# Second cross-attention of a two-block diffusion transformer: the first output product of a batch element issued behind the next element's sums and turned rows

## The chip, the cores and the metric

One core of one Trainium2 chip runs the whole program. The metric is the device time of one execution in microseconds, taken as the median of several executions. The profile shown is that of one execution of its own.

## What is computed

Eight batch elements of 512 tokens with 256 channels run through two transformer blocks. The part that this document is about is the cross-attention of the second block, with 16 heads of 64 channels and 64 context tokens for each element:

```python
cross_in = _adaln(x, cond, ln1_w, ln1_b, g1_w, g1_b, b1_w, b1_b)
ctx_n = _ln(context, ca_lnc_w, ca_lnc_b)
x = _attn(cross_in, ctx_n, ca_wq, ca_wkv, ca_wo, ca_bo) + x
...
q = _rope(_heads(xq @ wq), sq, cq);  k = _rope(_heads(ctx @ wk), sk, ck)
a = softmax(einsum('bhnd,bhmd->bhnm', q, k) * DH ** (-0.5))
o = einsum('bhnm,bhmd->bhnd', a, v).transpose(...).reshape(b, n, MID)
return o @ wo + bo
```

Everything is float32. Before this part come the first block and the second block's self-attention; after it comes the second block's feed-forward.

## The kernel before, in words

The order of the instructions on TensorE, VectorE, ScalarE and GpSimd is written out by hand: within `manual_schedule` (L1397) each of these engines issues its instructions in the order in which the Python code names them. Only the queue of SyncE, which starts nearly all transfers, is ordered by the compiler.

The cross-attention is `cross()` (L1334). It loops over the batch elements b and, in each, over eight steps j = 0..7. One pair of heads fills the 128 partitions, so there are eight pairs (NPAIR). The pieces that a step puts together are these:

- `queries(n)` (L1226): the queries of one pair, two matmuls of 512 columns into a PSUM tile, then rotary embedding in `rope_pair` (L840 to L844): three VectorE multiplications that read the PSUM tile (one at L840, two at L843), and one GpSimd addition that makes the query tile. The call at step j makes the queries for three steps ahead.
- `outer(b, pp)` (L1215): values times the output weight, copied to `vw` by ScalarE. With that, output weight and values are one factor, and the last product of the attention is probabilities times `vw`.
- `score(b, pp)` (L1236): the scores of two pairs, and their exponential on ScalarE (L1243) into a tile `p`. The probabilities are not yet divided by their sum.
- `sums(b, half)` (L1245): the sums of half the heads, four matmuls with a selecting matrix into one PSUM tile, a ScalarE copy `den` (L1253), and transfers (L1256, L1258) that bring them into a dense layout.
- `inverse(b, half)` (L1260): the reciprocal on VectorE (L1263), a transfer out (L1265), and eight transfers (L1270) that spread the reciprocals over the partitions as four tiles `rb`.
- `scaled(b, half)` (L1272): four multiplications of `p` by `rb` (L1277), two on GpSimd and two on VectorE in turn.
- `cross_out(b, t)` (L1290): the output of 128 tokens, eight matmuls of 256 columns with the eight scaled tiles `p` as weights and `vw` as the moving operand, through `out_tile` (L1279) and `project_tile` (L450). Products 0 and 1 share one PSUM tile, which is taken at product 0; products 2 and 3 share another. Behind product 1 and behind product 3 VectorE adds the tile to `x` (`add_to`, L461; L464).
- `turn(i)` (L1208): the normalised rows of the next element are turned by eight TensorE transposes in two groups, each into a PSUM tile of its own (L427), which ScalarE scales into `hT` (L428). The queries of the next element need `hT`.

The output products of element b-1 are issued in the steps of element b: product 0 and sums and turn at step 4, product 1 at the head of step 5, product 2 at step 6, product 3 at step 7. The scaling of the second half of b-1 is issued at step 3.

PSUM tiles of one bank come from `bank_x()` (L106), which goes round four banks by a counter: the single bank of tag D, the single bank of tag O, and twice tag X, which has two banks. Every `queries`, `outer`, `sums` and every group of `turn` takes one tile from it, and so do products 0 and 2. A tile can be taken only when what its bank held before has been read; the framework makes TensorE wait for that reader. For tag X the framework hands out the one of the two banks that has been given back first. Scores have four banks of their own (tag S).

```python
def bank_x():
    turns[0] += 1
    n = turns[0] % (2 + len(extra))
    if n < len(extra):
        return extra[n]()          # bank_d, bank_o
    return psum.tile([P, 512], F32, tag="X", name="ps_X", bufs=2)
```

Of the kernel before, what the change touches and what calls it, by code (L numbers as in the profile page):

```python
# [85 lines left out]
def fast_path(ctx: ExitStack, tc: tile.TileContext, a: dict, out: bass.AP):  # L86
# [334 lines left out]
    def transposed(pool, z, b, am, bm, bufs=2):  # L421

        hT = pool.tile([P, 2, N], F32, tag="hT", name="hT", bufs=bufs)
        for k in range(2):
            ps = bank_x()
            for t in range(NT):
                nc.tensor.transpose(ps[:, t * P : (t + 1) * P], z[:, t, k * P : (k + 1) * P], ident)  # L427
            nc.scalar.activation(hT[:, k, :], ps, AF.Identity, bias=bm[:, k, b : b + 1], scale=am[:, k, b : b + 1])  # L428
        return hT
# [512 lines left out]
    def load_kb(b):  # L942
        for i in range(4):
            r = slice(32 * i, 32 * i + 32)
            nc.sync.dma_start(kvs[b % 2][0][r, :, i % 2, :], k_d[r, :, b, :])

    def load_vb(b):
        for e in range(2):
            r = slice(64 * e, 64 * e + 64)
            nc.sync.dma_start(kvs[b % 2][1][r, :, e, :], v_d[r, :, b, :])  # L950
# [236 lines left out]
    with tc.tile_pool(name="ph5", bufs=2) as wk:  # L1187
# [9 lines left out]
        def rows_(i, n=None):  # L1197

            if i < 2 * B:
                b = i % B  # L1200
                if not n:
                    pieces[i] = normed_in_pieces(nk, b, EPS1, lambda z: turned_rows.update({i: z}))
                for piece in pieces[i] if n is None else pieces[i][n : n + 1]:
                    piece()
                if n in (None, 2):
                    add_row(b, row("ffb2" if i // B else "cabo"))

        def turn(i):  # L1208
            if i < 2 * B:
                am, bm = ((a1, b1), (a2, b2))[i // B]  # L1210
                turned_rows[i] = transposed((nk, wk)[i % 2], turned_rows[i], i % B, am, bm, 1)
# [3 lines left out]
        def outer(b, pp):  # L1215

            s = ss[b]
            if pp == 0:
                s["vw"] = wk.tile([P, NPAIR, D], F32, tag="vw", name="vw")
            ps = bank_x()  # L1220
            for i in range(2):
                p = 2 * pp + i
                mm(ps[:, i * D : (i + 1) * D], kvs[b % 2][1][:, p, :, :].rearrange("p e k -> p (e k)"), w_co[:, p, :])
            nc.scalar.copy(s["vw"][:, 2 * pp : 2 * pp + 2, :], ps.rearrange("p (i d) -> p i d", i=2))

        def queries(n):  # L1226
            b, p = divmod(n, NPAIR)
            if b == B:
                return
            ps = bank_x()  # L1230
            for k in range(2):
                mm(ps, w_cq[:, k, p * P : (p + 1) * P], turned_rows[b][:, k, :], k == 0, k == 1)
            ss[b][p] = q = wk.tile([P, N], F32, tag="q", name="q", bufs=7)
            rope_pair(wk, ps[:, None, :], rope_c[:, None, :], rope_s2[:, None, :], [P, 1, N], q[:, None, :])

        def score(b, pp):  # L1236
            s = ss[b]
            ps = bank_s()
            for i in range(2):
                p = 2 * pp + i  # L1240
                mm(ps[:, i, :], kvs[b % 2][0][:, p, :, :].rearrange("p e k -> p (e k)"), s[p])
            s["p", pp] = pr = wk.tile([P, 2, N], F32, tag="p", name="p", bufs=8)
            nc.scalar.activation(pr, ps, AF.Exp, scale=HD1 ** -0.5)  # L1243

        def sums(b, half):  # L1245

            s = ss[b]
            d = bank_x()
            for j in range(4):
                p = 4 * half + j  # L1250
                mm(d[32 * j : 32 * j + 32, :], sel0, s["p", p // 2][:, p % 2, :])
            den = wk.tile([P, N], F32, tag="den", name="den", bufs=1)
            nc.scalar.copy(den, d)  # L1253
            dd = dram.tile([4, 2, N], F32, tag="den5", name="den5")
            for e in range(2):
                nc.sync.dma_start(dd[:, e, :], den.rearrange("(j r) n -> j r n", j=4)[:, e, :])  # L1256
            s["rec", half] = rec = wk.tile([P, 8 * N // P], F32, tag="rec", name="rec")
            nc.sync.dma_start(rec, flat(dd))  # L1258

        def inverse(b, half):  # L1260
            s = ss[b]
            rec = s["rec", half]
            nc.vector.reciprocal(rec, rec)  # L1263
            rd = dram.tile([4, 2, N], F32, tag="rec5", name="rec5")
            nc.sync.dma_start(flat(rd), rec)  # L1265
            check(rec)
            for j in range(4):
                s["rb", j] = rb = wk.tile([P, N], F32, tag="rb", name="rb", bufs=4)
                for e in range(2):
                    nc.sync.dma_start(rb[64 * e : 64 * e + 64, :], rd[j, e : e + 1, :].to_broadcast([64, N]))  # L1270

        def scaled(b, half):  # L1272
            s = ss[b]
            for j in range(4):
                p = 4 * half + j
                pr = s["p", p // 2][:, p % 2, :]
                (nc.gpsimd, nc.vector)[p % 2].tensor_tensor(pr, pr, s["rb", j], ALU.mult)  # L1277

        def out_tile(b, t, lhsT, w):  # L1279
            s = ss[b]  # L1280
            if t % 2 == 0:
                s["ps"] = bank_x()
            project_tile(s["ps"], t % 2, lhsT, w, 8, t)
            if b == B - 1 and w is w_f2 and t > 1:
                x = xs[b][:, t, :]
                nc.vector.tensor_tensor(x, s["ps"][:, (t % 2) * D : (t % 2 + 1) * D], x, ALU.add)
            elif t % 2:
                add_to(b)(t // 2, s["ps"].rearrange("p (j d) -> p j d", j=2))

        def cross_out(b, t):  # L1290
            out_tile(b, t, lambda k: ss[b]["p", k // 2][:, k % 2, :], ss[b]["vw"])
# [42 lines left out]
        def cross():  # L1334
            LEAD = 3
            for n in range(LEAD):
                queries(n)
                if n:
                    outer(0, n - 1)
            for z in kvs[1]:  # L1340
                nc.gpsimd.memset(z, 0.0)
            for b in range(B):
                for j in range(NPAIR):
                    if j % 2 == 0:
                        queries(NPAIR * b + j + LEAD)
                        score(b, j // 2)
                    if b and j in (5, 6):
                        cross_out(b - 1, j - 4)
                    if j % 2:
                        queries(NPAIR * b + j + LEAD)  # L1350
                    if j < 2:
                        for pp in (2 * j, 2 * j + 1) if b else (2 + j,):
                            outer(b, pp)
                    if b:
                        if j == 0:
                            scaled(b - 1, 0)
                        if j == 1:
                            inverse(b - 1, 1)
                        if j == 3:
                            scaled(b - 1, 1)  # L1360
                        if j in (4, 7):
                            cross_out(b - 1, j - 4)
                    if j == 2 and b + 1 < B:
                        load_kb(b + 1)
                        load_vb(b + 1)
                    if j == 4:
                        sums(b, 0)
                        turn(b + 1)
                    if j > 4:
                        rows_(b + 2, j - 5)  # L1370
                    if j == 6:
                        inverse(b, 0)
                    if j == 7:
                        sums(b, 1)
# [22 lines left out]
        with tc.manual_schedule(engines={ENG.PE, ENG.DVE, ENG.Activation, ENG.Pool}):  # L1397
            cross()
            return feed_forward()
# [865 lines left out]
```

## Time and profile before

| what | us |
|---|---|
| median of 3 runs (lowest, highest) | 2419.1 (2417.03, 2423.43) |
| the profiled execution, its own time | 2413.91 |
| span of the profile | 2411.8 |
| TensorE busy in the span | 2379.0 |
| from the first product of element 0 (issued in element 1) to the first product of element 6 (issued in element 7), start to start | 257.7 |

The granted TensorE clock was 0.998 of full speed. In the profile a matmul in float32 appears as two records. The groups of the output products carry the name `ps_O<-vw,p` or `ps_X<-vw,p`, by the bank they write, the sums `<-p,sel`, the transposes `<-ident,z`, and the queries `<-hT,w_ca_wq`. Their line is L116, the helper that issues every matmul, or L427 for transposes. A number in square brackets in the timeline is the idle time of the engine ahead of an instruction, with what ended it.

### The profile page before, as it was taken

How to read it: one execution, taken by the hardware profiler on the slowest of the kernel's cores; microseconds unless marked ns; L12 is line 12 of the kernel's file. 1: busy time of each engine (PE TensorE's matmuls, PEld its weight loads, DVE VectorE, ACT ScalarE, POOL GpSimd, SP SyncE). 2: the span in 40 equal slices, each digit the busy share in tenths (PEclk: the TensorE clock that was granted, in tenths of full speed). 3: DMA queues.
4: the chain of work that ended last, by engine and by line, in shares of the span. 5: the costliest groups of instructions: out<-in, count | busy, mean ns of one | idle time of the engine just before them, and what ended most of it. 6: DMA issues, size and time to landing. Idle time of an engine off the chain costs nothing.

```text
span 2411.8 us, 28553 instructions
## 1 busy us (share of the span) xinstructions
PE 2379.0 (99%) x10964; PEld 1158.8 (48%) x10964; DVE 1139.5 (47%) x2115; ACT 889.2 (37%) x1118; POOL 966.5 (40%) x588
## 2 busy tenths in 40 slices
PE   9999999999999999999999999999999999999998
PEld 4333544544545633434343444444445556567665
DVE  4564534434345344555454555545445656651110
ACT  4665545545442134333333333333342212221221
POOL 4563323323201046555555554646453445441110
PEclk9999999999999999999999999999999999999999
DMA  5130000000002001000101010100023212210000
GB/s 184 33 107 11 16 15 13 16 14 6 12 11 92 0 1 32 14 24 10 28 10 28 10 28 10 28 10 26 30 67 95 77 58 68 64 56 31 18 22 20
DMA packets 84897, 84.07 MB, mean 35 GB/s; under 512 B 42656, under 2 KB 59792, under 8 KB 84752
## 3 DMA queue, kind: packets, MB, share of 16 engines
q1 hardware_dynamic: 83208, 78.99, 11.0%
q8 instruction: 88, 1.44, 0.2%
q0 software_dynamic: 640, 2.10, 0.2%
q10 hardware_dynamic: 904, 1.07, 0.2%
q14 instruction: 57, 0.47, 0.1%
HBM read 72.09 MB, written 10.04 MB: 34 GB/s over the span
## 4 chain that ended last, share of the span: by engine, by line
PE 87%; DVE 4%; POOL 3%; issue 3%; DMA 1%; ACT 1%; SPq 1%; POOLq 0%; DVEq 0%; ACTq 0%
PE ps_X L116 36%; PE ps_S L116 22%; PE ps_D L116 13%; PE ps_O L116 13%; PE ps_X L427 1%; DMA rb<-rec 1%; DVE t L843 1%; POOL x L448 1%; DVE sm L1039 1%; POOL p L1277 1%; ACT p L590 0%; PE ps_X L610 0%; POOL var L561 0%; DVE t L1000 0%; SPq L1270 0%
## 5 line engine op out<-in xcount | busy, mean ns | idle before, releaser
L116 PE MATMUL ps_S<-q,k 32*128 32x512 f32 (+1 forms) x3072 | 425.6, 623 | 5.5 <-ACT p L590 3.4
L1020 ACT ACTIVATE p<-ps_S 128x1024 f32<-128x1024 f32 x256 | 250.8, 1022 | 459.7 <-PE ps_S L116 450.3
L590 ACT ACTIVATE p<-ps_S 128x1024 f32<-128x1024 f32 x256 | 248.3, 1022 | 171.6 <-PE ps_S L116 170.3
L116 PEld LDWEIGHTS ps_S<-q,k 32*128 32x128 f32 (+1 forms) x3072 | 148.7, 183 | 244.8 <-issue 155.5
L1039 DVE TENSOR_TENSOR sm<-sm,p 128x1024 f32<-128x1024 f32 x128 | 252.1, 2028 | 0.1
L999 DVE TENSOR_TENSOR t<-ps_X,rope_c 128x512 f32<-128x512 f32 x126 | 87.0, 690 | 341.0 <-PE ps_X L116 341.0
L1002 POOL TENSOR_TENSOR q<-t 128x512 f32<-128x512 f32 x32 | 65.5, 2047 | 294.3 <-DVE t L1000 294.3
L182 POOL TENSOR_TENSOR rstd<-rstd,mhalf 128x4 f32<-128x4 f32 x49 | 51.2, 1044 | 293.6 <-DVE rstd L181 292.6
L844 POOL TENSOR_TENSOR q<-t,t 128x512 f32<-128x512 f32 x72 | 94.9, 1319 | 172.6 <-DVE t L843 171.6
L116 PE MATMUL ps_X<-hT,w 128*128 128x512 f32 x328 | 151.0, 597 | 0.5 <-DVE t L780 0.5
L1035 POOL TENSOR_TENSOR sm<-p 128x1024 f32<-128x1024 f32 x64 | 149.7, 2364 | 1.9 <-ACT p L1020 1.9
L1085 POOL TENSOR_TENSOR oT<-oT,rb 128x512 f32<-128x512 f32 x63 | 128.9, 2065 | 19.6 <-DMA rb<-rec_d 19.6
L116 PE MATMUL ps_O<-p,v 128*64 128x512 f32 x512 | 134.9, 605 | 0.0
L116 PE MATMUL ps_D<-p,v 128*64 128x512 f32 x512 | 131.6, 592 | 0.0
L116 PE MATMUL ps_O<-p,h 128*32 128x512 f32 x1024 | 129.5, 609 | 0.6 <-ACT p L590 0.6
L621 POOL TENSOR_TENSOR attn<-attn,gate 128x256 f32<-128x256 f32 x32 | 23.3, 727 | 250.7 <-DVE attn L619 250.7
L116 PE MATMUL ps_X<-w_sa_wv,hT 128*128 128x512 f32 x256 | 118.0, 604 | 0.0
L1002 POOL TENSOR_TENSOR k<-t 128x512 f32<-128x512 f32 x32 | 40.7, 1272 | 192.8 <-DVE t L1000 192.8
L116 PE MATMUL ps_X<-hT,w_sa_wq 128*128 128x512 f32 x256 | 115.9, 595 | 0.0
L116 PE MATMUL ps_X<-w_sa_wo,oT 128*128 128x256 f32 x512 | 114.5, 382 | 0.1
L116 PE MATMUL ps_X<-hT,w_sa_wk 128*128 128x512 f32 x248 | 114.6, 605 | 0.0
L116 PE MATMUL ps_S<-hT,w_ff_w 128*128 128x512 f32 x256 | 111.3, 593 | 0.0
(286 smaller groups left out, 3663.6 us busy)
## 6 DMA issues: line engine op xcount, KB each, us to landing
rb<-rec SPq DMA_DIRECT2D x128, 128.0 KB
rb<-rec_d SPq DMA_DIRECT2D x124, 128.0 KB
rb<-rec SPq DMA_DIRECT2D x16, 256.0 KB
out_dram<-x SPq DMA_DIRECT2D x15, 256.0 KB
x<-in_x_dram SPq DMA_DIRECT2D x7, 512.0 KB
gate<-modd SPq DMA_DIRECT2D x24, 128.0 KB
k_d<-q POOLq DMA_DIRECT2D x8, 256.0 KB, 2.4
v_d<-v SPq DMA_DIRECT2D x8, 256.0 KB
```

The source lines that it names most:

```text
L116: nc.tensor.matmul(o, lhsT, rhs, start=start, stop=stop)
L182: nc.gpsimd.tensor_tensor(r[:, :n], r[:, :n], mhalf[:, :n], ALU.pow)
L427: nc.tensor.transpose(ps[:, t * P : (t + 1) * P], z[:, t, k * P : (k + 1) * P], ident)
L448: nc.gpsimd.tensor_tensor(xs[b], xs[b], r[:, None, :].to_broadcast([P, NT, D]), ALU.add)
L590: nc.scalar.activation(pr[u], pss[u], AF.Exp, scale=HD0 ** -0.5)
L844: nc.gpsimd.tensor_tensor(dst, t1, t2, ALU.add)
L999: nc.vector.tensor_tensor(c, ps, rope_c, ALU.mult)
L1002: nc.gpsimd.tensor_tensor(r[0], ec, os, ALU.subtract)
L1020: nc.scalar.activation(pr, pss[u], AF.Exp, scale=HD1 ** -0.5)
L1035: nc.gpsimd.tensor_tensor(sm, s["p", g, 0, u], s["p", g, 1, u], ALU.add)
L1039: nc.vector.tensor_tensor(s["sm", g, u], s["sm", g, u], s["p", g, t, u], ALU.add)
L1085: eng.tensor_tensor(o, o, s["rb", g, u], ALU.mult)
```

## The change

Product 0 of element b-1 moves, within step 4 of element b, from ahead of `sums(b, 0)` and `turn(b + 1)` to behind them. Product 1 stays at the head of step 5 and so comes straight behind it. No instruction is added or taken away, and all other pieces keep their places. This holds for the seven elements b = 1..7; the products of the last element are issued in `feed_forward()` and are as they were.

```diff
                         if j == 3:
                             scaled(b - 1, 1)
-                        if j in (4, 7):
-                            cross_out(b - 1, j - 4)
+                        if j == 7:
+                            cross_out(b - 1, 3)
                     if j == 2 and b + 1 < B:
                         load_kb(b + 1)
                         load_vb(b + 1)
                     if j == 4:
                         sums(b, 0)
                         turn(b + 1)
+                        if b:
+                            cross_out(b - 1, 0)
                     if j > 4:
                         rows_(b + 2, j - 5)
```

## The prediction, on record before the result was known

> **What bounds the kernel now.** I read first the busy times, then TensorE's waits in the stage of the change (1825 to 2165 us), then the timeline of one element, because what the change is worth is decided there.
>
> ```profile
> PE 2379.0 (99%) x10964; PEld 1158.8 (48%) x10964; DVE 1139.5 (47%) x2115; ACT 889.2 (37%) x1118; POOL 966.5 (40%) x588
> ```
>
> TensorE is busy in 99% of the span and everything else in less than half: a microsecond that TensorE stalls is a microsecond of the kernel, unless it was waiting there anyway. The waits of TensorE in the stage (total, times, longest):
>
> ```profile
> PE ps_O L116 <- DVE x L464: 2.6, 3, 0.9
> PE ps_O L116 <- POOL p L1277: 2.1, 5, 0.9
> PE ps_X L116 <- DVE t L843: 1.7, 1, 1.7
> PE ps_X L116 <- POOL p L1277: 1.1, 4, 0.5
> ```
>
> Two waits recur. Product 0 waits for the scaled tiles (`p L1277`), and something behind product 1 waits for VectorE's addition to `x` (L464). Matmul ends are modelled, so I size both by start times. The timeline of element 2, TensorE first, then VectorE:
>
> ```profile
> 1929.64 1.88 PE L116 MATMUL ps_S<-q,kv 128*128 128x512 f32 x4
> 1931.36 1.89 PE L116 MATMUL ps_X<-vw,p 128*128 128x256 f32 x8
> 1933.43 2.48 PE L116 MATMUL ps_X<-vw,p 128*128 128x256 f32 x8 [0.18 <-POOL p L1277]
> 1935.83 1.07 PE L116 MATMUL ps_D<-p,sel 128*32 128x512 f32 x8
> 1936.83 0.66 PE L427 MATMUL ps_O<-ident,z 128*128 128x128 f32 x4
> 1937.42 0.63 PE L427 MATMUL ps_X<-ident,z 128*128 128x128 f32 x4
> 1937.89 3.62 PE L116 MATMUL ps_X<-vw,p 128*128 128x256 f32 x16
> 1941.34 1.88 PE L116 MATMUL ps_X<-hT,w_ca_wq 128*128 128x512 f32 x4
> ```
> ```profile
> 1931.55 0.70 DVE L1277 TENSOR_TENSOR p<-p,rb 128x512 f32<-128x512 f32 x1 [1.25 <-DMA rb<-rec]
> 1933.51 1.64 DVE L1277 TENSOR_TENSOR p<-p,rb 128x512 f32<-128x512 f32 x1 [1.26 <-DMA rb<-rec]
> 1935.18 0.69 DVE L840 TENSOR_TENSOR t<-ps_X,rope_c 128x512 f32<-128x512 f32 x1
> 1935.89 1.39 DVE L843 TENSOR_TENSOR t<-ps_X,rope_s 64x512 f32<-64x512 f32 x2
> 1941.54 0.69 DVE L464 TENSOR_TENSOR x<-ps_X,x 128x512 f32<-128x512 f32 x1 [4.27 <-PE ps_X L116]
> ```
>
> To be seen: product 0 (16 records) takes 4.47 us from its start to the start of the sums, product 1, which waits for nothing, 3.45 us; so product 0 stalls 1.02. And VectorE is late here. Its scaling waits for the `rb` transfers, and behind it in the queue stands the rotary embedding (L840, L843) of the step's own queries, whose PSUM tile is read out only at 1937.28, although TensorE filled it before 1929.64.
>
> **What the Trainium skill says.** "PSUM — Partial Sum Buffer", section "PSUM bank collisions raise a hardware error": accesses of two engines to a bank must be kept apart by semaphores, by bank and not by address; so a new tile in a bank waits for the last reader of the old one. The trace agrees: at element 1 the queries at 1899.13 in bank O start 0.15 us after the addition that read bank O ended (1898.98). "TensorE: Matmul & The Clock Gate", section "The mechanism": matmuls start and end in program order; so a matmul that waits for a bank holds up all behind it. The trace shows no matmul overtaking. "Perfetto Trace Analysis", section "Matmuls": independent groups should rotate through PSUM banks so that the evacuation of one overlaps the next group; here the rotation is where the change bites. "SBUF — State Buffer", section "SBUF: two separate sides": VectorE with two SBUF inputs and GpSimd exclude each other on a shared port. The trace agrees: L1277 on VectorE takes 0.70 above, and 1.64 beside GpSimd's L1277.
>
> **The change, part by part.** Let S be the start of product 0 before, for element b; all else is relative to it.
>
> (1) The order on TensorE. Sums take 1.00 us (1935.83 to 1936.83), the transposes 1.06 (to 1937.89). Moved ahead, they begin at S: their inputs are old, and they end at S+2.06. No DMA is moved past anything on TensorE; the `den` copy, its transfers and `hT` start about 4.4 us earlier, and nobody waits for them before (VectorE's L1263 for this half has no listed wait, and the queries that need `hT` come behind product 1), so I count nothing.
>
> (2) The wait for scaled tiles. The last of them is ready at S+3.79 typically (S+4.93 at element 1), and product 0 needs it at its eighth matmul, 7 x 0.43 = 3.0 us after its start. A start at S+2.06 would be late enough. This stall goes. Start to next start, product 0 takes 5.61, 4.47, 4.71, 4.47, 4.48, 4.80, 4.46 us in elements 1 to 7; less 3.45 each that is 8.9 us.
>
> (3) The bank. This is the part that decides. `bank_x` goes round four banks. From the fourth tile back before step 4 the takers are: the last `outer`, queries of step 2, of step 3, of step 4; then before the change: product 0, sums, transposes 1, transposes 2. So the last transposes reuse the bank of step 4's queries, at S+6.06 in element 2, when VectorE has just done with it. After the change it is sums, transposes 1, transposes 2, product 0: **product 0 takes the bank of the queries of step 4**. In the trace those queries write D in odd elements, where product 0 would then be the D tile, and X in even ones, where of the two X banks the sums get the one given back first. Sums and transposes get banks read out before S (the queries of step 3 by S-1.06, S-0.44 at element 1).
>
> So product 0 can start only at E+0.15, where E is the end of the last L843 for the queries of step 4, and 0.15 is the hand-over measured above. From the VectorE timelines, E is S+7.06, 5.92, 6.15, 5.92, 5.92, 4.69, 5.91. What makes E is not moved: VectorE's queue has scaling, then L840 and two L843 (2.1 us together), in the same order, and the scaling waits for `rb`. TensorE thus stands still from S+2.06 to S+6.07 typically, 4.0 us, and product 0 with its 3.45 us lies wholly behind it, where before most of it lay beside VectorE's lateness. Behind it on TensorE wait product 1, the next queries and the scores, so all of the kernel.
>
> Product 1 then ends at E+0.15+6.90; before, it ended at S+T+2.06+3.45, with T the times of (2). The difference is E+1.54-T: 2.99, 2.99, 2.98, 2.99, 2.98, 1.43, 2.99, in all **19.3 us lost**.
>
> (4) The other bank. In odd elements product 0 and 1 held O, and the queries of step 5 came round to O and waited for the addition: product 1 takes 4.49 to its next start there instead of 3.45, in elements 1, 3 and 5 (element 7 has no further queries). That is 3 x 1.04 = **3.1 us gained**, since these queries now get the bank of the sums, read out long before. In even elements they waited for nothing already (1941.34, ahead of the addition at 1941.54).
>
> (5) What follows. VectorE sits idle 4.27 us ahead of the addition in each element; the delay shifts TensorE and VectorE together from there, so the chain of reciprocal and `rb` for the next element starts as late as its products, and the loss comes again in each element without growing. Nothing else is added.
>
> Sum: 19.3 - 3.1 = 16.2 us slower. On the profiled execution that is 2413.9 + 16.2 = 2430.1. That execution lies 5.2 us under the median of the runs, so on the median I forecast 2419.1 + 16.2 = **2435.3 us**. A measurement of this kernel can tell about 0.3% (7 us) from no change.
>
> **Bounds.** E is the one uncertain time. At best `rb` lands as early as in element 6 and no L1277 of VectorE meets one of GpSimd: with 0.70 + 2.1 from S+1.4, E is S+4.2, the loss 1.3 an element, and 7 x 1.3 - 3.1 = 6 us: 2425. At worst the sums, not product 0, get the late X bank in three even elements, and product 0 comes another 2.06 us later: +6.2, 2441.5.
>
> **The rivals.** *Faster*: product 0's bank is free in time, because the bank is handed out otherwise than I count. Then (2) and (4) stand alone: 8.9 + 3.1 = 12.0 us gained, 2407.1. For it speaks that TensorE's listed waits name the scaled tiles and not this bank; against it, that before the change transposes 2, which hold the bank by my count, start 0.14 us behind E in element 2 and 0.59 behind transposes 1, but only 0.50 behind them in element 6 (2108.16 to 2108.66), where E is early: a tenth of the bank's wait shows. It decides at E = S+2.93 (S+3.97 where (4) helps): below, the change gains. E is 4.69 at the least. *No change*: E comes down by some 2.4 us on average, for instance since transfers land earlier behind a longer stall, and loss and gain cancel: 2419. Against it: reciprocal and `rb` issue lie ahead of the stall. *Much slower*: the stall feeds back into the order of SyncE's queue, which the compiler makes anew, and `rb` comes later by 2 us an element: 14 us more, 2449.
>
> **Chances.** Forecast 0.81, faster rival 0.07, no change 0.05, much slower 0.07. The range runs from under the lower bound to above the upper one with some room for the median's own scatter of 3 us: 2424 to 2443. Faster by over 0.3%: 0.07. Within 0.3%: 0.06. Slower by over 0.3%: 0.87.
>
> **What would show it.** Right: in each element TensorE idles about 4 us ahead of the first `<-vw,p` behind the transposes, put down to `DVE t L843`; product 0 then takes 3.45 us; the sums start at S; in odd elements product 0 writes D, and the wait for `DVE x L464` is gone; the step from one element's first product to the next grows by 2 to 3 us from about 42.8. Wrong: an idle time there under 1 us, or one put down to `POOL p`, or VectorE's L843 of step 4 ending well ahead of S+5.

## The result, and the profile after

Nine executions of the changed kernel have a median of 2437.3 us, nine of the kernel before 2419.37; the ratio, taken over all executions and not over the two medians (which would give 1.0074), is 1.0057, with a 95% interval of 1.0036 to 1.0077, so the change costs 9 to 19 us. The gains and losses of whole executions below are taken from such ratios. The profiled execution of the changed kernel took 2430.07 us, with a span of 2427.8 against 2411.8. Executions of the changed kernel range from 2425.5 to 2439.1 us, in step with their mean granted TensorE clock: 0.995 at 2425.5, 0.992 at 2429 to 2430, 0.989 to 0.990 at 2437 to 2439.

The waits of TensorE in the stage, after (total, times, longest):

```profile
PE ps_D L116 <- DVE t L843: 17.4, 5, 4.9
PE ps_X L116 <- DVE t L843: 1.7, 1, 1.7
PE ps_D L116 <- ACT hT L428: 0.4, 1, 0.4
```

The waits for the scaled tiles and for the addition are gone from the list. In their place stands a wait of bank D for VectorE's L843, the read of a query tile: 17.4 us in five times, one of which (0.9) was there before. The timeline of TensorE in element 1, after:

```profile
1887.11 1.06 PE L116 MATMUL ps_O<-p,sel 128*32 128x512 f32 x8
1888.10 1.09 PE L427 MATMUL ps_X<-ident,z 128*128 128x128 f32 x8
1894.11 9.76 PE L116 MATMUL ps_D<-vw,p 128*128 128x256 f32 x32 [4.92 <-DVE t L843]
1903.71 1.88 PE L116 MATMUL ps_O<-hT,w_ca_wq 128*128 128x512 f32 x4
```

Sums and transposes start at once; products 0 and 1 (32 records) stand on bank D and wait 4.92 us. VectorE, there:

```profile
1890.98 0.86 DVE L1277 TENSOR_TENSOR p<-p,rb 128x512 f32<-128x512 f32 x1 [1.20 <-DMA rb<-rec]
1891.87 0.69 DVE L840 TENSOR_TENSOR t<-ps_D,rope_c 128x512 f32<-128x512 f32 x1
1892.58 1.39 DVE L843 TENSOR_TENSOR t<-ps_D,rope_s 64x512 f32<-64x512 f32 x2
```

The last read of `ps_D` ends at 1893.97, and product 0 starts 0.14 us later. But the two products then take 9.60 us to the next start, not the 6.9 of twice 3.45. The same view of element 2, after:

```profile
1935.96 1.06 PE L116 MATMUL ps_X<-p,sel 128*32 128x512 f32 x8
1936.96 0.66 PE L427 MATMUL ps_D<-ident,z 128*128 128x128 f32 x4
1937.45 0.60 PE L427 MATMUL ps_O<-ident,z 128*128 128x128 f32 x4
1937.89 7.14 PE L116 MATMUL ps_X<-vw,p 128*128 128x256 f32 x32
1944.86 1.88 PE L116 MATMUL ps_X<-hT,w_ca_wq 128*128 128x512 f32 x4
```

Here nothing waits. The readers of the two X banks, ScalarE for the sums and VectorE for the step's queries:

```profile
1937.21 0.59 ACT L1253 COPY den<-ps_X 128x512 f32<-128x512 f32 x1
1939.81 0.69 DVE L840 TENSOR_TENSOR t<-ps_X,rope_c 128x512 f32<-128x512 f32 x1
```

VectorE reads the step's queries from an X bank only from 1939.81 on, when product 0 has been writing its own X bank for 1.9 us: so the two are different banks. Tag X has only two, so product 0 holds the bank of the sums, which ScalarE had copied out at 1937.80.

The long time of element 1 is explained by a stage view (stretch, its length, busy time of PE, PEld, DVE, ACT, POOL, each with its instructions, then the granted TensorE clock):

```profile
1889.20:1892.60 3.40, 0.00 (x0) 0.00 (x0) 2.15 (x4) 1.10 (x2) 1.29 (x2) 1.00 0.21 67
1892.60:1899.40 6.80, 5.29 (x13) 4.24 (x14) 1.35 (x2) 0.00 (x0) 1.27 (x1) 0.50 0.01 2
1899.40:1902.80 3.40, 3.40 (x17) 3.01 (x16) 0.00 (x0) 0.00 (x0) 0.00 (x0) 1.00 0.00 0
```

TensorE does nothing for 3.4 us at full clock, then the clock is halved for 6.8 us: 13 records in that stretch, 5.3 us of them busy, against 17 in the 3.4 us behind it.

All else can be read from one number per element: the time from S, the start of the first of sums, transposes and products behind the scores of step 4, to the queries behind product 1 (scores in element 7). From there to the next S it takes 32.15 to 32.25 us before and 32.25 after, so these seven times hold the difference:

| element | 1 | 2 | 3 | 4 | 5 | 6 | 7 | sum |
|---|---|---|---|---|---|---|---|---|
| before | 12.16 | 9.98 | 11.25 | 9.98 | 11.03 | 10.18 | 9.97 | 74.6 |
| after | 16.61 | 8.90 | 15.47 | 8.90 | 15.41 | 8.90 | 15.37 | 89.6 |

The sum is 15.0 us of the 16.0 by which the span grew.

### The profile page after: what moved, and what is told of

The parts are those of the page before. It is cut to its first block, busy times and chain, and to the rows that moved or that the text cites. A ratio compares the mean times of both kernels' runs of the same rounds, so it can differ in the third digit from the quotient of the medians.

```text
span 2427.8 us, 28558 instructions
## 1 busy us (share of the span) xinstructions
PE 2382.7 (98%) x10964; PEld 1168.0 (48%) x10964; DVE 1140.0 (47%) x2115; ACT 889.8 (37%) x1118; POOL 966.9 (40%) x588
## 4 chain that ended last, share of the span: by engine, by line
PE 87%; DVE 4%; issue 3%; POOL 2%; DMA 2%; ACT 1%; SPq 1%; DVEq 0%; POOLq 0%; ACTq 0%
PE ps_X L116 36%; PE ps_S L116 22%; PE ps_D L116 15%; PE ps_O L116 12%; DMA rb<-rec 1%; PE ps_X L427 1%; SPq L1270 1%; DVE t L843 1%; POOL var L561 1%; DVE sm L1039 1%; PE ps_X L610 0%; ACT p L590 0%; DVE t L1000 0%; POOL x L448 0%; DVE t L840 0%
```

## The experiments

The theory after the result: in odd elements product 0 waits for the bank of step 4's queries; the idle time makes the clock drop to half for the products behind it; in even elements the X bank of the sums is handed on to product 0, and the move gains there what it frees. Rivals: product 0 is late because of where it stands in the order, whatever its bank; something else that alternates between elements; a halved clock that has nothing to do with the idle time. Each experiment is judged by its ratio to the kernel before, run on the same chip, and by the seven times of its profile. The span alone is a poor witness, since half-clock stretches ahead of the stage come and go in any of these kernels.

**Another bank for product 0, in the changed order.**

```diff
-                s["ps"] = bank_x()
+                s["ps"] = bank_s()[:, 0, :] if t == 0 and b < B - 1 and w is not w_f2 else bank_x()
```

> The changed order, but products 0 and 1 of elements 0 to 6 take half of a scores tile (tag S, free at step 4) in place of a tile from the round of four, so product 0 no longer stands on the bank of step 4's queries. S is the start of the first of sums, transposes and products behind the scores of step 4. Theory (the bank decides): the 4.0 us idle ahead of product 0 in the odd elements is gone, the TensorE clock is not halved in the stage, and from S to the next queries it takes 8.9 us in every element (as in the even elements of the changed kernel) against 9.97 to 12.16 before; 7 x 8.9 = 62.3 against 74.6 us, so 12 us faster than before: 2407, ratio 0.995. Rival (product 0 is late because it stands behind VectorE's lateness whatever its bank, or because of its scaled tiles): an idle time of some 4 us stays, named after the scaled tiles, 2425 or more.

Measured: 2406.56 us, ratio 0.9951 (0.9933 to 0.9968), and 8.84 us in each of the seven elements. Element 1:

```profile
1893.25 1.06 PE L116 MATMUL ps_O<-p,sel 128*32 128x512 f32 x8
1894.25 1.09 PE L427 MATMUL ps_X<-ident,z 128*128 128x128 f32 x8
1895.18 7.07 PE L116 MATMUL ps_S<-vw,p 128*128 128x256 f32 x32
1902.09 1.88 PE L116 MATMUL ps_D<-hT,w_ca_wq 128*128 128x512 f32 x4
```

No idle time, and no half-clock stretch in the stage. The order of the change is a gain of 12 us (0.0049 of 2419) once its product stands on a free bank. The rival of the mere order falls, and this version beats both kernels. Since its product 0 takes no tile from the round, the other takers meet other banks than in the changed kernel too; the time is 8.84 us in every element all the same.

**The round moved on by two.** One line, `turns[0] += 2`, ahead of the loop of `cross()` in the changed kernel.

> The changed kernel with the round of four banks moved on by two ahead of the loop, so that product 0 holds D in the even elements (2, 4, 6) and X in the odd ones. No work is added or removed. Theory (only the element whose product 0 holds D waits; on X it gets the bank that the sums have just given back): the long S-to-queries times of 15.4 us move to the even elements, the odd ones take 8.9; 3 x 15.4 + 4 x 8.9 = 81.8 against 74.6 before: 7 us slower than before, 8 less than the changed kernel; if the clock is not halved, equal to before. Rival (something in the odd elements other than the bank, such as the buffers of keys, turned rows or scores, which also alternate): the long elements stay odd, and the time is the changed kernel's.

Measured: 2423.79 us, ratio 1.0026 (1.0013 to 1.0040); the seven times are 8.91, 15.38, 8.90, 15.36, 8.91, 14.74, 8.91, sum 81.1. The long elements are now the even ones. Element 2:

```profile
1938.88 1.09 PE L427 MATMUL ps_X<-ident,z 128*128 128x128 f32 x8
1943.86 9.56 PE L116 MATMUL ps_D<-vw,p 128*128 128x256 f32 x32 [3.89 <-DVE t L843]
```

What makes an element long goes with the round, by which product 0 gets bank D, and not with the parity of keys, turned rows or scores.

**The idle time filled.** In the changed kernel, n = 9 matmuls that nobody reads, ahead of product 0 in odd elements.

```diff
+                        if b % 2:
+                            idle = bank_s()
+                            for _ in range(9):
+                                mm(idle[:, 0, 0:256], ident, rope_c[:, 0:256])
                         if b:
                             cross_out(b - 1, 0)
```

> The changed kernel, with nine extra matmuls (identity times a 256-column table, 0.43 us each, 3.9 us in all, into a free scores tile that nobody reads) between transposes and product 0 in the odd elements: they fill the idle time of TensorE and leave the wait for the bank as it is. The output is not affected. Theory (the idle time of 4 to 5 us makes the granted clock drop to half, and products 0 and 1 then run at half speed): no half-clock stretch in the stage, products 0 and 1 take 6.9 us and not 9.2 to 9.8, from S to the next queries 13.9 us in element 1 and 13.0 in elements 3, 5 and 7 against 15.4 to 16.6, so some 10 us less than the changed kernel's profile: about 2420 on the profile, median 2424. Rival (the halving has another cause, such as time or load): unchanged, or slower where the extra matmuls overrun.

Measured: 2424.53 us, ratio 1.0022 (1.0009 to 1.0035). Odd elements take 13.91, 12.95, 12.97, 12.72, even ones 8.90, sum 79.3. Element 3:

```profile
1974.90 4.05 PE L116 MATMUL ps_S<-rope_c,ident 128*128 128x256 f32 x18
1978.94 7.14 PE L116 MATMUL ps_D<-vw,p 128*128 128x256 f32 x32
1985.93 1.88 PE L116 MATMUL ps_O<-hT,w_ca_wq 128*128 128x512 f32 x4
```

Product 0 starts at S+5.97, as in the changed kernel (S+5.99), but the two products take 6.99 us and the clock is full throughout the stage. More work on TensorE made the program faster than the changed kernel (ratio 1.0022 against 1.0057, and against 1.0048 in the second series below): the halved clock comes from the idle time.

**Half of it filled.** The same with n = 4.

> The changed kernel with four extra matmuls (0.43 us each, 1.7 us in all) between transposes and product 0 in the odd elements, in place of nine: they leave 2.3 us of idle time ahead of product 0 (3.3 in element 1), and the wait for the bank as it is. If the clock is halved only when TensorE idles through a whole stretch of 3.4 us (the unit in which all half-clock stretches of the traces come: 3.4, 6.8, 10.2), there is no halving in elements 3, 5, 7 and perhaps one in element 1, and the time is that of nine extra matmuls, 2424. If a partly idle stretch is enough, the halving stays, 2430 or more.

Measured: 2425.64 us, ratio 1.0015 (1.0004 to 1.0027). The profiled execution has half-clock stretches of 6.8 us in element 1 and 3.4 us in element 5, none in 3 and 7; the odd elements take 16.82, 12.96, 14.66, 11.72. Element 5 goes against the expectation, since its idle time is 2.2 us:

```profile
2072.90:2076.30 3.40, 1.23 (x6) 1.02 (x6) 2.10 (x4) 0.00 (x0) 0.81 (x1) 0.99 0.06 13
2076.30:2079.70 3.40, 3.40 (x10) 2.68 (x9) 0.00 (x0) 0.00 (x0) 0.46 (x1) 0.51 0.00 0
```

In the stretch ahead of the drop TensorE was busy for 1.23 of 3.4 us. A wholly idle stretch is not needed; that option of the expectation fell. It is the profile that shows this: the time lies between the two that were expected, and its ratio cannot be told from that of nine extra matmuls.

**The changed kernel once more.**

> The changed kernel unaltered, to see the half-clock stretches of another execution. The runs so far fall into three groups (2425.5, 2429 to 2430, 2437 to 2439 us) with mean granted clocks of 0.995, 0.992 and 0.990. Theory: the wait for the bank is the same in every execution and the groups differ in the number of half-clock stretches alone, by 2.2 to 2.7 us each; the S-to-queries time in odd elements is then either 13.0 or 15.4 (one more in element 1), and 8.9 in even ones, whatever the clock. Rival: the wait itself varies between executions, with the landing of the reciprocals.

Measured: 2431.09 us, ratio 1.0048 (1.0034 to 1.0063). Even elements take 8.90 to 8.91; odd ones 16.15, 14.97, 11.82, 14.62. Element 5 shows no halved clock and a shorter wait:

```profile
2074.34 7.14 PE L116 MATMUL ps_D<-vw,p 128*128 128x256 f32 x32 [2.75 <-DVE t L843]
```

So both vary between executions: the clock, and the wait too (product 0 starts at S+7.40, 6.30, 4.84, 5.96). The theory's claim that the clock alone differs fell, and these ten executions don't fall into the three groups. The landing of the reciprocals, which the rival named, is only part of it. In element 1 VectorE's second multiplication starts 0.57 us later behind S than in the first profile, because its `rb` lands later. In element 5 it starts only 0.15 us earlier but takes 0.69 us instead of 1.68, and that is most of the 1.14 us by which product 0 comes earlier.

**The sums alone moved ahead.** `sums`, then product 0, then `turn`.

> Product 0 stands behind the sums but ahead of the transposes, so the fourth taker, which reuses the bank of step 4's queries, is again the second group of transposes. Theory: product 0 starts at S+1.0 on a bank read out long ago and its eighth matmul comes at S+4.0, when the scaled tiles are just ready (S+3.9), so that stall goes; the second transposes then wait about 1 us for VectorE's L843 (E+0.15 = S+6.1 against S+5.0); from S to the next queries 10.0 us, 11.1 in element 1, 8.9 where VectorE is early; no idle time near 4 us and no halved clock; the queries behind product 1 no longer wait for the addition in odd elements. 70 against 74.6 us: 4 to 5 us faster than before, 2415. Rival (no bank): 8.9 everywhere, 2407; rival (product 0 behind the sums is what costs): slower than before.

Measured: 2413.01 us, ratio 0.9976 (0.9965 to 0.9986), 6 us faster. The seven times are 10.68, 8.88, 10.13, 8.88, 9.91, 8.95, 9.90, sum 67.3. Element 3:

```profile
1984.42 0.60 PE L427 MATMUL ps_X<-ident,z 128*128 128x128 f32 x4
1986.07 0.63 PE L427 MATMUL ps_D<-ident,z 128*128 128x128 f32 x4 [1.05 <-DVE t L843]
```

The wait follows the fourth taker, now the second transposes, and again only where that is D: in even elements, where it is X, nothing waits, which the expectation had not seen.

**The bank alone.** The first diff in the order of before.

> The order of before, with products 0 and 1 of elements 0 to 6 in half of a scores tile. Theory: the wait of the odd elements' queries for the addition goes (3 x 1.04 = 3.1 us), the second transposes no longer wait for VectorE (a tenth each), product 0 still waits for its scaled tiles. From S to the next queries 10.99, 9.85, 10.08, 9.85, 9.86, 10.18, 9.85 = 70.7 against 74.6 us: 4 us faster than before, 2414. The 8 us between this and the changed order with the same banks are then what the move itself brings. Rival (the bank of product 0 matters only in the changed order): no change.

Measured: 2416.6 us, ratio 0.9984 (0.9972 to 0.9995), 4 us faster; 10.70, 9.86, 10.65, 9.86, 9.86, 10.18, 9.85, sum 71.0. The wait for the addition is gone from the odd elements, and the one for the scaled tiles is there. With the bank free, the move itself is worth the rest: 71.0 against 61.9, 9 us.

## Why the prediction was right, and where it was not

The forecast of 2435.3 us came within 2 us of the median, and the 2430.1 us for the profiled execution met the measured 2430.07. That closeness was luck: a term of step (3) was 10.9 us too high, a term of 10.3 us was missing, and the two misses cancel. The direction was no luck: with the clock held up, the wait for the bank in the odd elements still costs more than the move gains (ratio 1.0022 with the idle time filled). But that alone, some 5 us, would have lain at the very foot of the range.

- **Steps (1) and (2)** held. Sums start at S, transposes at S+1.00, and nothing waits for scaled tiles. The move with a free bank gave 12 us where the faster rival's sum, (2) and (4), said 12.0. The rival's arithmetic was right. Its premise, a free bank, held in the three even elements and failed in the four odd ones.
- **Step (3), odd elements:** the mechanism held, and E to within 0.31 us. It was S+6.86, 5.84, 5.83 and 5.82 in elements 1, 3, 5 and 7, against 7.06, 6.15, 5.92 and 5.91 taken from before, and product 0 starts 0.14 us behind it in element 1.
- **Step (3), even elements, failed.** The prediction counted the X tag as part of a strict round: of the two X banks the sums would get the older, product 0 that of step 4's queries. But the sums now stand ahead of product 0, and their X bank is given back (at 1937.80 in element 2) before that of the queries (1941.91), so product 0 gets the sums' bank. Predicted for elements 2, 4 and 6: +2.99, +2.99, +1.43; measured -1.08, -1.08, -1.28: 10.9 us too much.
- **A term was missing:** the halved clock behind the idle time. The two products took 9.41 to 9.60 us in odd elements instead of 6.91 (8.84 - 1.93 in the version with another bank), which is 2.5 to 2.7 each and 10.3 us in all. The prediction had looked at a 4 us stall on the most loaded engine and priced it at its length. The Trainium skill has what was needed: "TensorE: Matmul & The Clock Gate", section "HAM oscillation — how this bites in real kernels", says to leave no idle gap above some 3.4 us. The prediction drew on that page for the order of matmuls only.
- **Step (4)** held: the wait for L464 is gone in elements 1, 3 and 5, and the bank alone gives 4 us against 3.1 and the tenths of the transposes.
- **Step (5)** held: 32.25 us from the queries to the next S, in every element.
- **The signs:** the idle time put down to `DVE t L843`, bank D in the odd elements and the end of the wait for L464 all came. "In each element" and "3.45 us for product 0" did not, and they point to the two misses.

Worked out for the profiled execution: odd elements without the clock +8.2 (predicted 8.8), clock +10.3 (predicted 0), even elements -3.4 (predicted +7.4): 15.0, predicted 16.2.

What stays open: why single executions differ in the landing of the reciprocals and in the length of VectorE's multiplications, and what decides how the clock's stretches lie against the idle times of an execution. A version in which product 0 takes the bank of the queries in the even elements too wasn't tried.

## What to carry to other kernels

When a step that takes a PSUM tile from a rotation is moved, write down who takes each bank next and when its last reader ends; the moved step inherits another step's reader, and here that, with the halved clock behind it, turned a gain of 12 us into a loss of 14. A tag with two banks doesn't follow a round of fixed places, so work out from the readers in the trace which bank is handed out. And price a stall of TensorE with what follows it: it can be paid again in half-speed matmuls (2.2 us were enough in one case here, 2.75 us were not in another), so either give the step a bank of its own or keep TensorE busy.

## What the runs showed of the hardware

The half-clock stretches come in multiples of 3.4 us (3.4 and 6.8 in this stage). The Trainium skill, "TensorE: Matmul & The Clock Gate", section "What's actually happening", tells of a window of 3413 ns that runs freely and of the slow clock after at least one idle window. The length agrees. The condition is wider here: cutting the nine traces into such windows in step with their own drops, every drop in this stage came at the end of a window in which TensorE was busy for 0.01 to 0.44 of the time, and no window in it with a busy share of 0.49 or more was followed by one. This holds for the stage alone. Far ahead of it the busy share does not decide: one window of 0.44 was followed by no drop, one of 0.50 was (the drop at 73.3 us after the change), and in each of the nine traces there is a drop behind a window of 0.91 (at 158.3 us before the change). Why is not known. In the stage, an idle time of 2.2 us was enough when it fell into one window (element 5 of the half-filled kernel), and one of 2.75 us was not when it lay across two (element 5 of the second execution). By the length of the two products over 6.91 us, a drop cost 1.8 to 3.1 us where it lasted 6.8 us, part of which was idle anyway, and 1.7 to 1.8 us where it lasted 3.4. The drop lasted 3.4 us in the three cases in which TensorE was busy through the whole of its first window, and 6.8 in the nine others.
